# The message stage of a four-layer graph network: high and low halves of the products in the same 96 columns, and Q's rows by a one-hot over 64 rows held twice

## The chip, the cores and the metric

The kernel runs on one core of one Trainium2 chip. The metric is the device time of one execution in microseconds; the kernel before takes 2623.59 us (median of 3 runs, 2621.11 to 2624.36). Times inside an execution come from the hardware profiler. Engines are named as the profile names them: PE (TensorE, its weight loads apart as PEld), DVE (VectorE), ACT (ScalarE), POOL (GpSimd) and SP (SyncE, which here only issues transfers).

## What is computed

The input is a graph of 3125 nodes with 96 features and 100000 edges, sorted by destination, with 4 attributes per edge. Four layers are added to `x` one after the other, each on `relu(layernorm(x))`. The change concerns the third, whose message part is this (cut from the reference):

```python
dst = jnp.minimum((3125 * jax.random.uniform(key3, (100000,)) ** 2.0).astype(jnp.int32), 99999)
_o = jnp.argsort(dst, stable=True)
...
def _mlp(h, W, b, gamma, beta):
    h = jax.nn.relu(h @ W + b)
    mu = jnp.mean(h, axis=0)
    var = jnp.mean(jnp.square(h - mu), axis=0)
    return gamma * (h - mu) * jax.lax.rsqrt(var + EPS) + beta
node_feat = _mlp(x, W_node, b_node, g_node, beta_node)
edge_feat = _mlp(edge_attr, W_edge, b_edge, g_edge, beta_edge)
row, col = (edge_index[0], edge_index[1])
message = jnp.concatenate([x[row], x[col], edge_feat], axis=1)
message = _mlp(message, W_msg, b_msg, g_msg, beta_msg)
agg = jax.ops.segment_sum(message, col, num_segments=node_feat.shape[0])
return agg + node_feat
```

`row` is the source of an edge, `col` its destination. Destinations are denser at low node numbers, and sorted, so that consecutive edges have the same or neighbouring destinations.

## The kernel before

The first layers (edge preparation, ten hops of propagation, softmax aggregation) come ahead of the part that the change touches, and the last layer behind it. One exception: the edge preparation writes tables that the message stage reads later.

**Split numbers.** Products that must be nearly fp32 are made of fp16 numbers: a value is held as a high half and the low remainder. `split` writes both: ACT casts the value to fp16, DVE subtracts the cast from the value (the page's lines L369 and L370).

**Tables.** The message of an edge is relu(P[source] + Q[destination] + edge features x W3), where P and Q are the nodes' products with their parts of the weights. `Pt` and `Qt` hold them in memory, one row of 192 fp16 numbers per node: 96 high and 96 low ones.

**Quads and halves.** The edges are worked in `Q` = 98 quads of `QE` = 1024, each of two halves (`PER` = 2), each half of four chunks (`HC` = 4) of 128 edges. For a quad `load_quad` issues on SP's queue: the 128 rows of `Qt` from the quad's first destination on, into `qg` (the row number comes from the table `rows` in a register); the edge attributes `et`; and `rlb`, every edge's destination relative to the quad's first one, spread over all 128 partitions. `rows_hot` (L741) compares `rlb` with the partition number `part`, which gives the one-hot `ohT` (destination row by edge). `cols_hot` makes the transposed one, `oh`, for the sums.

**Gathers.** `gather_rows(i)` issues on POOL four indirect transfers (L736), each of which brings the `Pt` rows of 128 edges into one of six buffers of a half, `pgs`. A buffer is rewritten when the half six places before has been read by PE.

**One half.** `edge_features` multiplies the attributes on PE into `ef`; ACT's relu gives `eh`, DVE's L757 the rest `el`. `messages(i)` then makes, for each chunk, four matmuls in one PSUM tile `pre` of 192 columns: `eh` times `W3h` (high and low side by side, 192 columns, L766), `el` times the high half (96 columns, L767), `ohT` times `qg` (192, L768), and the identity times the gathered rows (192, L769). The tile holds four chunks at a stride of 256 fp32 columns, which is two PSUM banks, and there are two such tiles. ACT copies the low 96 columns to `mt` (L771), DVE adds the high ones (L772), makes the relu (L774, less the message at the mean, `cb`), and `split` puts both halves in one of four buffers `mms`. Two halves later `summed` multiplies the one-hot `oh` with them on PE (segment sums, L792) and the messages with themselves (their second moments for the normalisation, L794). After a quad's second half its sums go to memory from `sacc` (L797 to L799), and into the next quad's sum (L791).

**Order.** The whole stage is issued in an order written by hand (`manual_schedule`). In turn i: edge features of half i+1, sums of half i-2, messages of half i, `rows_hot` of the next quad in an even turn, `cols_hot` and `load_quad` (two quads ahead) and a piece of the node branch (`node_piece`) in an odd one, then the gathers of half i+5. Each engine runs its instructions in this order.

**Edge preparation.** Destinations relative to the quad's first are computed as `rl` on 98 partitions (a quad each) of 1024 edges; `rlh` is its cast to fp16 (L303), which `rl_d` keeps for `rlb`. `firsti` goes to `row_d`, from which `rows` is loaded. `lo` holds a base row of each group of edges, `rows` in this place the destinations. Sums in the columns of `over` count edges that don't fit the assumed layout; if any is above zero, another, general function does the work (`wide`).

Of the kernel before, what the change touches and what calls it, by code (L numbers as in the profile page):

```python
# [20 lines left out]
P = 128  # L21
N, D, E = 3125, 96, 100000
# [7 lines left out]
HC = 4  # L30
# [8 lines left out]
BN_EPS = 1e-5  # L39
K_HOPS, ALPHA, BETA = 10, 0.1, 0.9  # L40
Q, QE = 98, 1024
ROWS = 4
WIN = 20
PAD = WIN
# [10 lines left out]
def narrow(ctx: ExitStack, tc: tile.TileContext, a: dict, out: bass.AP, flag: bass.AP):  # L55


    nc = tc.nc
    V, S, G, T = nc.vector, nc.scalar, nc.gpsimd, nc.tensor

    const = ctx.enter_context(tc.tile_pool(name="const", bufs=1))
    dram = ctx.enter_context(tc.tile_pool(name="dram", bufs=1, space=DRAM))
# [3 lines left out]
    Qt = dram.tile([NP + P, 2 * D], F16, name="Qt")  # L66
# [2 lines left out]
    rl_d = dram.tile([Q * QE], F16, name="rl_d")  # L69
    srcT_d = dram.tile([P, Q * 8], I32, name="srcT_d")  # L70
    first_d = dram.tile([1, Q], F32, name="first_d")
    row_d = dram.tile([1, Q], I32, name="row_d")
    base_d = dram.tile([Q * ROWS], I32, name="base_d")
    ea_d = dram.tile([18, E], F16, name="ea_d")

# [4 lines left out]
    ident16 = const.tile([P, P], F16, name="ident16")  # L80
# [2 lines left out]
    V.memset(ones, 1.0)  # L83
    lane = const.tile([P, P], F16, name="lane")
    G.iota(lane, pattern=[[1, P]], base=0, channel_multiplier=0, allow_small_or_imprecise_dtypes=True)
    part = const.tile([P, 1], F32, name="part")
    G.iota(part, pattern=[[0, 1]], base=0, channel_multiplier=1, allow_small_or_imprecise_dtypes=True)
    top = const.tile([P, 1], F32, name="top")
    V.memset(top, -float(TOP))
    over = const.tile([P, 80], F32, name="over")  # L90
    V.memset(over, 0.0)
    where = [const]
# [47 lines left out]
    with tc.tile_pool(name="edges", bufs=1) as sp, tc.tile_pool(name="onehot", bufs=3) as hp, tc.tile_pool(name="handed", bufs=2) as hd, \  # L140
# [56 lines left out]
        w = sp.tile([Q, QE], F32, name="w")  # L197
# [102 lines left out]
        turned(rlT, rl)  # L300
        turned(srcT, sb)
        rlh = sp.tile([Q, QE], F16, name="rlh")
        V.tensor_copy(rlh, rl)  # L303
        nc.sync.dma_start(rl_d.rearrange("(q e) -> q e", q=Q), rlh)
        nc.sync.dma_start(rlT_d, rlT.rearrange("p q j -> p (q j)"))
        nc.sync.dma_start(srcT_d, srcT.rearrange("p q j -> p (q j)"))


        firsti = sp.tile([Q, 1], I32, name="firsti")
        V.tensor_copy(firsti, lo[:, 0:1])  # L310
        nc.sync.dma_start(row_d.rearrange("o q -> q o"), firsti)
        nc.sync.dma_start(first_d.rearrange("o q -> q o"), lo[:, 0:1])
        fr = sp.tile([P, Q], F32, name="fr")
        nc.sync.dma_start(fr, first_d.to_broadcast([P, Q]))
# [30 lines left out]
    def over_b(t, nb=NB):  # L345

        return t[:, None, :].to_broadcast([P, nb, D])
# [228 lines left out]
    nc.sync.dma_start(rlT, rlT_d)  # L576
    srow = where[-1].tile([P, Q * 8], I32, name="srow")
    nc.sync.dma_start(srow, srcT_d)
    rows = where[-1].tile([1, Q], I32, name="rows")
    nc.sync.dma_start(rows, row_d)  # L580
    li = where[-1].tile([P, P, 4], F16, name="li2")
    G.iota(li, pattern=[[1, P], [0, 4]], base=0, channel_multiplier=0, allow_small_or_imprecise_dtypes=True)  # L582
# [85 lines left out]
    with tc.tile_pool(name="msg", bufs=1) as lp, tc.tile_pool(name="gath", bufs=6) as gp, \  # L668
# [48 lines left out]
        st = {"acc": None}  # L717

        def load_quad(g):
            r0 = nc.values_load(rows[0:1, g:g + 1], engines=(mybir.EngineType.SP,), min_val=0, max_val=N - 1,  # L720
                                skip_runtime_bounds_check_because="a dst is a node")
            qg = gp.tile([P, 2 * D], F16, name="qg")
            nc.sync.dma_start(qg, Qt[bass.ds(r0, P), :])
            et = wp.tile([18, QE], F16, name="et", bufs=4)
            n = min(QE, E - g * QE)
            if n < QE:
                V.memset(et, 0.0)
            nc.sync.dma_start(et[:, :n], ea_d[:, g * QE:g * QE + n])
            rlb = rlbs[g % len(rlbs)]
            nc.sync.dma_start(rlb, bass.AP(tensor=rl_d.tensor, offset=rl_d.offset + g * QE, ap=[[0, P], [1, QE]]))  # L730
            quad[g] = [r0, qg, et, rlb]
# [6 lines left out]

        def rows_hot(g):
            ohT = wp.tile([P, QE], F16, name="ohT")  # L740
            V.tensor_scalar(ohT, quad[g][3], part, None, ALU.is_equal)  # L741
            quad[g].append(ohT)

        def cols_hot(g):
# [15 lines left out]
        def messages(i):  # L760
            r0, qg, et, rlb, ohT, oh = quad[i // PER]
            eh, el = half_[i]
            ps = p2.tile([P, HC, 256], F32, name="pre")[:, :, :2 * D]
            for c in range(HC):
                cs = slice(c * P, (c + 1) * P)
                T.matmul(ps[:, c, :], eh[:, cs], W3h, start=True, stop=False)  # L766
                T.matmul(ps[:, c, :D], el[:, cs], W3h[:, :D], start=False, stop=False)  # L767
                T.matmul(ps[:, c, :], ohT[:, i % PER * HC * P + c * P:i % PER * HC * P + (c + 1) * P], qg, start=False, stop=False)  # L768
                T.matmul(ps[:, c, :], ident16, pgs[i % len(pgs)][:, c, :], start=False, stop=True)  # L769
            t = wp.tile([P, HC, D], F32, name="mt")  # L770
            S.activation(t, ps[:, :, D:], AF.Copy)  # L771
            V.tensor_add(t, t, ps[:, :, :D])  # L772
            m = wp.tile([P, HC, D], F32, name="m")
            V.scalar_tensor_tensor(m, t, 0.0, over_b(cb, HC), ALU.max, ALU.subtract)  # L774
            for c in range(HC):
                first = E - (i * HC + c) * P
                for p0, pn in ((0, 32), (32, 32), (64, 64)) if first < P else ():
                    assert first <= p0 or first >= p0 + pn
                    if first <= p0:
                        V.memset(m[p0:p0 + pn, c, :], 0.0)  # L780
            mm = mms[i % len(mms)]
            split(mm[:, :, :D], mm[:, :, D + 2:], m)
# [720 lines left out]
```

## Time and profile before

| what | value |
|---|---|
| median of the runs | 2623.59 us |
| the profiled execution | 2623.51 us |
| its span, first to last instruction | 2621.6 us |
| mean granted TensorE clock | 0.813 |
| PE / DVE / ACT / POOL busy, share of the span | 75 / 59 / 37 / 31% |
| message stage, place in the span | about 1256 to 2455 us |
| gathers (L736) | 784, 992 ns each |
| messages' matmuls (L766 to L769) | 4 x 784 |

The page has numbered parts. Its second part cuts the span into 40 slices of 65.5 us; a digit is the busy share of a slice in tenths, and in the clock's row the granted clock in tenths of full speed. Its fifth part lists groups of instructions: line, engine, operation, output and inputs, shapes, count; then busy time and mean duration in ns; then how long the engine had been idle ahead of them and what ended most of that. A timeline gives start, duration, and in brackets the idle time ahead of an instruction with its releaser. Ends of matmuls are modelled, so starts are safer than ends. "issue" is time in which an engine waited for nothing that the profile shows.

### The profile page before, as it was taken

To read this page: it belongs to the slowest core of one execution; us is meant where nothing else is said; L and a number is where in the kernel's file an instruction comes from. 1 tells how busy PE (TensorE), PEld (TensorE's weight loads), DVE (VectorE), ACT (ScalarE), POOL (GpSimd) and SP (SyncE) were. 2 spreads that over 40 slices of the span, in tenths; PEclk is the share of its full clock that TensorE was granted. 3 is DMA by queue.
4 is the path that set the end of the run, shared out by engine and by line. 5 is a ranking of instruction groups with operands and counts; after the bars stand their busy time and mean duration, and the time that the engine had idled before them with its cause. 6 is when DMAs were issued, how large, how long until landed. Compare 5 with 4: busy or idle time off the path is not lost.

```text
span 2621.6 us, 43748 instructions
## 1 busy us (share of the span) xinstructions
PE 1975.0 (75%) x16190; PEld 1516.1 (58%) x16190; DVE 1540.0 (59%) x4164; ACT 959.6 (37%) x2332; POOL 819.6 (31%) x808
## 2 busy tenths in 40 slices
PE   0477777899999999998475566667677767667598
PEld 0222334788888899987354444445455555455488
DVE  2777999875656553877255454445444444445753
ACT  0398855469533311433132222222222222222340
POOL 4000000000000000000666566666666666666000
PEclk9789989999999999999556766765666665676699
DMA  2100000000000000000222222322222223232100
GB/s 66 55 24 1 1 1 1 5 9 10 9 10 10 10 21 2 19 21 18 61 66 67 52 67 65 71 65 70 64 70 66 70 65 70 64 70 66 29 2 21
DMA packets 101315, 100.65 MB, mean 38 GB/s; under 512 B 66285, under 2 KB 73206, under 8 KB 101090
## 3 DMA queue, kind: packets, MB, share of 16 engines
q1 hardware_dynamic: 73754, 54.78, 7.9%
q0 software_dynamic: 25088, 38.59, 7.4%
q10 hardware_dynamic: 2248, 4.40, 0.6%
q8 instruction: 128, 2.10, 0.3%
q14 instruction: 97, 0.79, 0.1%
HBM read 83.46 MB, written 14.21 MB: 37 GB/s over the span
## 4 chain that ended last, share of the span: by engine, by line
PE 44%; DVE 16%; issue 13%; ACT 9%; another core or an unknown queue 1%; DMA 0%; SPq 0%; DVEq 0%; ACTq 0%; POOL 0%; POOLq 0%
PE hop L380 19%; PE segs L792 4%; PE gram L794 3%; PE pre L769 3%; PE pre L768 3%; ACT x L524 3%; DVE u L370 3%; PE pre L766 3%; DVE mt L772 2%; DVE m L774 2%; PE ef L753 2%; ACT mt L771 2%; PE pre L767 1%; PE eps L513 1%; ACT A L437 1%
## 5 line engine op out<-in xcount | busy, mean ns | idle before, releaser
L736 POOL DMA_INDIRECT u<-Pt,srow x784 | 778.0, 992 | 550.8 <-issue 180.2
L380 PE MATMUL hop<-u,A 128*128 128x192 f16 (+1 forms) x6250 | 550.0, 247 | 2.3 <-DVE degs L474 1.4
L380 PEld LDWEIGHTS <-A 128*128 128x128 fp8e4 x6250 | 522.5, 98 | 47.4 <-issue 43.8
L792 PE MATMUL segs<-u,oh 128*128 128x194 f16 x784 | 225.8, 323 | 232.7 <-DVE ohT L741 139.4
L772 DVE TENSOR_TENSOR mt<-mt,pre 128x384 f32<-128x384 f32 x196 | 108.4, 553 | 478.9 <-ACT mt L771 345.6
L771 ACT ACTIVATE mt<-pre 128x384 f32<-128x384 f32 x196 | 96.1, 490 | 605.9 <-PE pre L769 249.6
L768 PE MATMUL pre<-qg,ohT 128*128 128x192 f16 x784 | 256.9, 328 | 25.6 <-issue 25.3
L769 PE MATMUL pre<-u,ident 128*128 128x192 f16 x784 | 258.5, 330 | 22.4 <-issue 21.4
L269 PE MATMUL cps<-hk,hl 128*128 128x500 f16 x784 | 232.7, 418 | 54.1 <-DVE hl L227 35.5
L794 PEld LDWEIGHTS <-u 128*97 128x97 f16 x784 | 137.2, 175 | 235.2 <-issue 231.5
L766 PE MATMUL pre<-W3h,eh 96*128 96x192 f16 x784 | 259.0, 330 | 15.4 <-issue 14.6
L227 DVE TENSOR_TENSOR hk<-ki,keyT 128x4000 f16<-128x4000 f16 x98 | 220.5, 2250 | 45.0 <-PE cps L269 27.5
L794 PE MATMUL gram<-u 128*97 128x194 f16 x784 | 228.2, 325 | 3.7 <-issue 3.5
L767 PE MATMUL pre<-W3h,el 96*128 96x96 f16 x784 | 204.8, 261 | 28.5 <-issue 25.5
L582 POOL IOTA li<- 128x512 f16 x1 | 1.2, 1185 | 680.2 <-ACT exs L500 680.2
L273 ACT ACTIVATE C<-cps 128x500 f32 x269 | 162.8, 605 | 93.2 <-PE cps L272 66.4
L369 ACT ACTIVATE u<-m 128x384 f16<-128x384 f32 x196 | 102.5, 523 | 243.5 <-DVE m L774 204.2
L370 DVE TENSOR_TENSOR u<-m,u 128x384 f16<-128x384 f32 x196 | 109.5, 559 | 115.6 <-issue 86.7
L269 PEld LDWEIGHTS <-hl 128*128 128x128 f16 x784 | 74.0, 119 | 167.6 <-DVE hl L227 76.4
L792 PEld LDWEIGHTS <-oh 128*128 128x128 f16 x784 | 101.5, 129 | 109.4 <-issue 109.4
L514 ACT ACTIVATE eps<-eps 96x512 f32<-96x512 f32 x196 | 106.3, 569 | 154.5 <-PE eps L513 146.0
L515 DVE BATCH_NORM_STATS2 x<-eps 96x6 f32<-96x512 f32 x196 | 134.2, 688 | 30.8 <-ACT eps L514 28.2
(308 smaller groups left out, 3244.3 us busy)
## 6 DMA issues: line engine op xcount, KB each, us to landing
h<-rl_d SPq DMA_DIRECT2D x98, 256.0 KB
u<-Pt,srow POOLq DMA_INDIRECT x784
qg<-Qt SPq DMA_DIRECT2D x98, 48.0 KB
Sd<-sacc SPq DMA_DIRECT2D x98, 48.0 KB
x<-ea_d SPq DMA_DIRECT2D x195, 18.0 KB
et<-ea_d SPq DMA_DIRECT2D x97, 36.0 KB
et<-in_edge_attr_T ACTq DMA_DIRECT2D x4, 390.6 KB
ea_d<-eh SPq DMA_DIRECT2D x8, 195.3 KB
```

Of the source, the lines that this page charges most:

```text
L227: V.tensor_tensor(t, pat[:, None, :, :].to_broadcast([P, s, n, c]), val[:, q, :].rearrange("p (s c) -> p s c", s=s)[:, :, None, :].to_broa ...
L269: T.matmul(ps, hl[:, j // 4, :, j % 4], hk[:, j // 2, :, j % 2], start=j == js[0], stop=n == 0 and j == js[-1])
L273: S.activation(C8[:, :, bass.ds(column_of(g), WIN)], ps, AF.Copy)
L370: V.tensor_sub(lo, t, hi)
L380: T.matmul(ps[:, i, :], table[:, k, c0 + (b0 + i) * P:c0 + (b0 + i + 1) * P], u[:, k, :], start=k == 0, stop=k == NB - 1)
L736: G.indirect_dma_start(out=pgs[i % len(pgs)][:, c, :], out_offset=None, in_=Pt, in_offset=bass.IndirectOffsetOnAxis(ap=srow[:, k:k + 1], a ...
L766: T.matmul(ps[:, c, :], eh[:, cs], W3h, start=True, stop=False)
L767: T.matmul(ps[:, c, :D], el[:, cs], W3h[:, :D], start=False, stop=False)
L768: T.matmul(ps[:, c, :], ohT[:, i % PER * HC * P + c * P:i % PER * HC * P + (c + 1) * P], qg, start=False, stop=False)
L769: T.matmul(ps[:, c, :], ident16, pgs[i % len(pgs)][:, c, :], start=False, stop=True)
L792: T.matmul(seg, oh[:, half, :, c], mm[:, c, :], start=half == 0 and c == 0, stop=last)
L794: T.matmul(gram, mm[:, c, :D + 1], mm[:, c, :], start=i == 0 and c == 0, stop=g == Q - 1 and last)
```

## The change

In `messages` the six products of a chunk, high or low, all go into the same 96 columns: `eh` times the high and the low half of `W3`, `el` times the high half, the one-hot times `qg`, the identity times the high and times the low gathered half. PSUM adds what the copy and the addition added before; `mt` is gone, and `m` reads `pre`, which is one bank for four chunks.

For Q's two halves in one matmul, `qg` holds 64 rows twice: the high halves in partitions 0 to 63, the low ones of the same rows in partitions 64 to 127, and the one-hot has a one in both places (`part_hw` counts 0 to 63 twice). Since 64 rows must do, each half of a quad has its own first row, so `qg` has two blocks, and four transfers of 64 x 96 numbers fill it; two rows per quad are loaded into registers. `rlh` is therefore relative to the half's first row, and an edge that lies 64 or more rows above it is counted in a new column of `over`. The gathers, the sums and the order of issue are as before.

```diff
+HW = 64
...
-    row_d = dram.tile([1, Q], I32, name="row_d")
+    row_d = dram.tile([1, 2 * Q], I32, name="row_d")
...
-    part = const.tile([P, 1], F32, name="part")
-    G.iota(part, pattern=[[0, 1]], base=0, channel_multiplier=1, allow_small_or_imprecise_dtypes=True)
+    part = const.tile([P, 2], F32, name="part")
+    G.iota(part, pattern=[[0, 2]], base=0, channel_multiplier=1, allow_small_or_imprecise_dtypes=True)
+    V.tensor_scalar(part[HW:, 1:2], part[HW:, 1:2], -float(HW), None, ALU.add)
+    part, part_hw = part[:, 0:1], part[:, 1:2]
...
-        V.tensor_copy(rlh, rl)
+        r2 = rlh.rearrange("q (t e) -> q t e", t=2)
+        V.tensor_sub(r2, rows.rearrange("q (a b) e -> q a (b e)", a=2),
+                     lo.rearrange("q (a b) -> q a b", b=2)[:, :, 0:1].to_broadcast([Q, 2, QE // 2]))
+        V.tensor_scalar(bad, rlh, float(HW), None, ALU.is_ge)
+        V.tensor_reduce(over[:Q, 5:6], bad, AX.X, ALU.add)
...
-        firsti = sp.tile([Q, 1], I32, name="firsti")
-        V.tensor_copy(firsti, lo[:, 0:1])
-        nc.sync.dma_start(row_d.rearrange("o q -> q o"), firsti)
+        firsti = sp.tile([Q, 2], I32, name="firsti")
+        V.tensor_copy(firsti, lo.rearrange("q (a b) -> q a b", b=2)[:, :, 0])
+        nc.sync.dma_start(row_d.rearrange("o (q t) -> (o q) t", t=2), firsti)
...
         def load_quad(g):
-            r0 = nc.values_load(rows[0:1, g:g + 1], engines=(mybir.EngineType.SP,), min_val=0, max_val=N - 1,
-                                skip_runtime_bounds_check_because="a dst is a node")
-            qg = gp.tile([P, 2 * D], F16, name="qg")
-            nc.sync.dma_start(qg, Qt[bass.ds(r0, P), :])
+            _, r = nc.values_load_multi_w_load_instructions(
+                rows[0:1, 2 * g:2 * g + 2], engines=(mybir.EngineType.SP,), min_val=0, max_val=N - 1,
+                skip_runtime_bounds_check_because="a dst is a node")
+            r0 = r[0]
+            qg = gp.tile([P, 2, D], F16, name="qg")
+            for t in range(2):
+                for k in range(2):
+                    nc.sync.dma_start(qg[k * HW:(k + 1) * HW, t, :], Qt[bass.ds(r[t], HW), k * D:(k + 1) * D])
...
-            V.tensor_scalar(ohT, quad[g][3], part, None, ALU.is_equal)
+            V.tensor_scalar(ohT, quad[g][3], part_hw, None, ALU.is_equal)
...
-            ps = p2.tile([P, HC, 256], F32, name="pre")[:, :, :2 * D]
+            ps = p2.tile([P, 512], F32, name="pre")[:, :HC * D].rearrange("p (c d) -> p c d", c=HC)
+            pg = pgs[i % len(pgs)]
             for c in range(HC):
                 cs = slice(c * P, (c + 1) * P)
-                T.matmul(ps[:, c, :], eh[:, cs], W3h, start=True, stop=False)
-                T.matmul(ps[:, c, :D], el[:, cs], W3h[:, :D], start=False, stop=False)
-                T.matmul(ps[:, c, :], ohT[:, i % PER * HC * P + c * P:i % PER * HC * P + (c + 1) * P], qg, start=False, stop=False)
-                T.matmul(ps[:, c, :], ident16, pgs[i % len(pgs)][:, c, :], start=False, stop=True)
-            t = wp.tile([P, HC, D], F32, name="mt")
-            S.activation(t, ps[:, :, D:], AF.Copy)
-            V.tensor_add(t, t, ps[:, :, :D])
+                o = ohT[:, i % PER * HC * P + c * P:i % PER * HC * P + (c + 1) * P]
+                for j, (t, w) in enumerate(((eh[:, cs], W3h[:, :D]), (eh[:, cs], W3h[:, D:]), (el[:, cs], W3h[:, :D]),
+                                            (o, qg[:, i % PER, :]), (ident16, pg[:, c, :D]), (ident16, pg[:, c, D:]))):
+                    T.matmul(ps[:, c, :], t, w, start=j == 0, stop=j == 5)
             m = wp.tile([P, HC, D], F32, name="m")
-            V.scalar_tensor_tensor(m, t, 0.0, over_b(cb, HC), ALU.max, ALU.subtract)
+            V.scalar_tensor_tensor(m, ps, 0.0, over_b(cb, HC), ALU.max, ALU.subtract)
```

More of the change, by code (lines that the diff above doesn't have):

```diff
@@ L578, in narrow @@
     nc.sync.dma_start(srow, srcT_d)
-    rows = where[-1].tile([1, Q], I32, name="rows")
+    rows = where[-1].tile([1, 2 * Q], I32, name="rows")
     nc.sync.dma_start(rows, row_d)
```

## The prediction

> **What bounds the kernel now.** I began with the page: the sliced busy rows first, then the groups.
>
> ```profile
> PE   0477777899999999998475566667677767667598
> POOL 4000000000000000000666566666666666666000
> PEclk9789989999999999999556766765666665676699
> ...
> L736 POOL DMA_INDIRECT u<-Pt,srow x784 | 778.0, 992 | 550.8 <-issue 180.2
> L792 PE MATMUL segs<-u,oh 128*128 128x194 f16 x784 | 225.8, 323 | 232.7 <-DVE ohT L741 139.4
> L772 DVE TENSOR_TENSOR mt<-mt,pre 128x384 f32<-128x384 f32 x196 | 108.4, 553 | 478.9 <-ACT mt L771 345.6
> L771 ACT ACTIVATE mt<-pre 128x384 f32<-128x384 f32 x196 | 96.1, 490 | 605.9 <-PE pre L769 249.6
> L768 PE MATMUL pre<-qg,ohT 128*128 128x192 f16 x784 | 256.9, 328 | 25.6 <-issue 25.3
> L767 PE MATMUL pre<-W3h,el 96*128 96x96 f16 x784 | 204.8, 261 | 28.5 <-issue 25.5
> ```
>
> A slice is 65.5 us. POOL works only in slices 20 to 37: this is the message stage (about 1256 to 2455 us of the span), the only place where the change has much to do. Its 1200 us are 98 quads of 1024 edges, two halves of 512 each. No engine is full there, and the granted clock falls to 0.5 to 0.7. Next I asked for the engines' busy times in stretches of the stage, and then for the timelines of one quad, POOL, ACT, PE in turn:
>
> ```profile
> 1850.00:2000.00 150.00, 104.33 (x658) 76.45 (x656) 74.39 (x143) 40.84 (x91) 100.50 (x102) 0.64 0.29 68
> 2000.00:2150.00 150.00, 103.44 (x655) 75.20 (x654) 71.84 (x139) 39.85 (x89) 99.64 (x101) 0.65 0.28 66
> ...
> 2002.55 0.94 POOL L736 DMA_INDIRECT u<-Pt,srow  x1 [1.82 <-PE pre L769]
> ...
> 2011.61 0.95 POOL L736 DMA_INDIRECT u<-Pt,srow  x1 [0.31 <-issue]
> 2014.43 0.94 POOL L736 DMA_INDIRECT u<-Pt,srow  x1 [1.87 <-PE pre L769]
> ...
> 2002.57 0.49 ACT L771 ACTIVATE mt<-pre 128x384 f32<-128x384 f32 x1 [4.76 <-PE pre L769]
> ...
> 2014.44 0.49 ACT L771 ACTIVATE mt<-pre 128x384 f32<-128x384 f32 x1 [4.77 <-PE pre L769]
> ...
> 2009.96 0.37 PE L769 MATMUL pre<-u,ident 128*128 128x192 f16 x1
> ```
>
> (Columns of the stretches: length, then PE, PE load, DVE, ACT, POOL busy, clock, DMA share, GB/s.) Three things are to be seen. First, a quad lasts 2014.43 - 2002.55 = 11.88 us, and POOL fills 10.01 of it with eight gathers (2002.55 to 2012.56, a gather each 1.25 us), then stands for 1.87 us. It stands because the message rows go into six buffers: the next gather may start only when L769 has read the buffer. Second, that L769 had been executed long before: the even half's last one ended at 2010.33 by the trace, and ACT's copy, which waits for nothing else, began at 2014.44, 4.11 us later. Both engines were released in the same moment, 1.9 us after POOL's last gather ended. So completions of PE reach the waiting engines late while gathers are being issued, and in a bunch once POOL stands. Third, the loop behind that moment, from the chain of waits of this window:
>
> ```profile
> 2003.10 0.57 DVE mt L772
> 2003.66 0.02 issue
> 2003.68 0.56 DVE m L774
> 2004.24 0.59 issue
> 2004.83 0.56 DVE u L370
> 2005.39 0.45 DVE ohT L741
> 2005.83 0.80 issue
> 2006.64 0.32 PE segs L792
> ```
>
> From copy to copy the work is: mt copied and added (1.11 us), m, its high and low halves, then the sums of that half on PE (from 2006.64) and the next even half's messages (2007.88 to 2010.33). That is 7.8 us; the rest of the 11.88 is the late signal.
>
> **What the Trainium skill says.** "TensorE: Matmul & The Clock Gate", "Back-to-back issue gap": start to start is the column count over 1.2 GHz while cold and over 2.4 GHz plus about 2.5 ns when warm. The trace agrees for the cold state: 192-column matmuls start 160 ns apart and 96-column ones 80 to 90 ns (2012.82 to 2012.90), the weight load hidden. "VectorE: DVE Perf Modes", "Why PSUM operands drop a tier": with a PSUM operand fp32 runs at the single rate. L774 works on fp32 and three operands already; L772, with one operand in PSUM, takes 553 ns against L774's 560, so I cost m's new source at nothing. "DMA: Bandwidth & Descriptors", "Specifications": below 512 B a transfer is under line rate. The old Q rows (384 B) and the new ones (192 B) are both below; the page counts 66285 of 101315 packets under 512 B already, at a DMA share of 0.28 to 0.29. No section I found bears on signals of PE held up by gathers.
>
> **The change part by part.**
>
> *The copy and the add go.* 196 x 490 = 96.1 us of ACT and 196 x 553 = 108.4 us of DVE. Neither engine is full (40 and 72 of 150 us), so only their place on the chain counts: m starts where the copy started, 1.11 us earlier (2002.57 instead of 2003.68) in each half.
>
> *Fewer columns, more instructions.* A chunk goes from 192+96+192+192 = 672 columns in four matmuls to 6 x 96 = 576 in six. At the cold spacing a half's messages take 24 x 0.08 = 1.92 us instead of 4 x 0.56 = 2.24: 0.32 us less, if an instruction costs only its columns. PE gets 16 pairs of load and matmul more per quad (1568 of each in all). An unknown is what a pair costs where completions are held up; below, rival S.
>
> *One PSUM bank for a half instead of two, still two buffers.* They come free after m rather than after the add, which is the same moment or 0.5 us earlier. Nothing.
>
> *Signals.* In the compiled program PE's messages carry fewer completions: most of the plain ones sat on ohT and ident matmuls of the 192-column form and fall away (per quad about 21 before, 11 after; POOL still needs one per gather). If each costs a turn at a narrow place, this helps; waits on PE rise by two per quad. Below nothing, up to rival G.
>
> *Q rows.* Per quad four loads of 64 x 192 B instead of one of 128 x 384 B, and six more SP instructions. SP issues at 2006.61, 2008.35 and 2009.07 in this quad and rests otherwise: a qg issue has a median of 26 ns, a register move 29 ns, so 6 x 0.03 = 0.2 us on an idle queue, with load_quad two quads ahead. The row loads of rlb stand behind them by that 0.1 to 0.2 us; rows_hot needs them more than 10 us later. Cost nothing; if the cover were gone, 0.2 us per quad, 20 us. DMA bytes are the same; 128 more small packets beside some 1024 of gathers per quad.
>
> *One-hot and edges phase.* L741 is the same instruction with another scalar. In the edges phase the cast of 0.69 us (L303) becomes a subtraction (nearest row 1.22 us, L296), and a compare (0.69, L288) and a reduce (1.22, L287) are new: +2.4 us on DVE, which is near full there, so I count all of it, plus 0.1 us for the small part column. The flag that it fills rises only if a half spans 64 rows or more: destinations are 3125 u² with u uniform and sorted, so the widest half is the last, 3125 x (1 - (1 - 0.00512)²) = 32 rows. So it isn't raised.
>
> *The sum.* The chain of a quad is shorter by 1.11 + 0.32 = 1.43 us: the even half's first gather buffer is read at about F + 4.9 instead of F + 6.1 (2008.65 against the release at 2002.55), and all four by F + 6.3 instead of 7.8. POOL runs out at F + 10.0 as before. Whether the completion comes before that decides. Half of the stop is what I take as likeliest: a signal that is ready earlier and has fewer beside it gets through in some quads before POOL stands and in others not. The stop is 1.87 - 0.30 = 1.57 us beyond the ordinary pause between gathers; with it gone a quad would be 10.31 us. Half is 0.8 us in 83 regular quads: -66 us. In the ten or so quads with a node piece (1410 to 1530; POOL busy 69 of 120 us against 100 of 150) PE waits for DVE and ACT and the late signal is not the limit, so the chain counts in full: 10 x 1.43 = -14; the first quads, where the first 28 gathers are issued without a reader, and the last two: -4. Edges +2.5. Sum -82 us against the profiled execution's 2623.51 us (span 2621.6), which is 0.1 us from the median of 2623.59: 2542 us.
>
> **The rivals.**
>
> *G, POOL becomes the only bound.* The stop goes in all regular quads: 83 x 1.57 = -130, with the other terms -146: 2478 us. For it: the completions halve and come 1.4 us earlier. Against: held-up completions have been seen to pass only when POOL stands, and if it no longer stands they may pile up. Chance 0.24.
>
> *P, the stop stays.* The quad is eight gathers and the time to drain, whatever the chain does; only node pieces, first and last quads gain: -16 us, 2607 us. For it: release comes at a fixed 1.9 us after the last gather (2000.73 to 2002.55, 2012.56 to 2014.43), though L769 had ended 4 us earlier. Then a shorter chain is worth nothing. If the edges phase or Q loads take a little more, it ends within 5 us of before (a third of this case). Chance 0.21.
>
> *S, slower: PE is paid by the instruction.* Where completions are held up, PE's matmuls stall as well (L766 at 2013.40 was followed by L767 at 2014.10: 0.70 us for an 80 to 160 ns step). Mean durations show how little the columns count: 261 ns for 96 (L767), 328 for 192 (L768). If a half's messages are worth 24 x 0.261 = 6.3 us instead of 12 x 0.329 + 4 x 0.261 = 5.0, PE loses 1.3 us per half against the 1.1 us won by the copy and the add; both halves lie in PE's order one behind the other, 2.6 lost against 2.2 won, and PE's 8.2 us busy per quad become 10.8, more than the 10.3 of POOL. One 0.7-us stall more per quad beside that, for the two added waits, makes about +0.9 to +1.1 us per quad: 2623.5 + 95 = 2720 us. It decides from about 0.23 us per added pair. Without that stall it would be +0.4 us per quad, 2662 us. Chance 0.22.
>
> **How the numbers follow.** Half of the stop gone 0.33, G 0.24, P 0.21, S 0.22. The time is that of the likeliest, 2542 us; its own range is 2500 to 2585 (a quarter to nearly all of the stop gone, the unknown costs within). For eight in ten the range goes from 2460 (G with a little more in the node pieces) to 2655 (S where PE keeps most of its cover). A change within 0.2% (5 us) is about what a measurement of this kernel can't tell from none. Faster: 0.33 + 0.24 + two thirds of P = 0.71; same 0.07; slower 0.22.
>
> **What would show it.** In the changed kernel's POOL timeline the idle time before every eighth gather: 1.8 us again means P, 0.3 means G, a mixture or an intermediate value my forecast. m's start against the last ident matmul of its half gives the late signal (4.1 us now). PE's busy time per 150 us above 125 and 96-column matmuls starting more than 0.2 us apart would be S. If the time changes outside 1256 to 2455 us by more than 5 us, my reading of the edges phase was wrong.

## The result and the profile after

The changed kernel is slower: 2651.11 us (median of 4 runs, 2647.15 to 2655.02) against 2622.35 us for the kernel before, a ratio of 1.011 with a 95% interval of 1.0092 to 1.0128. The forecast was 2542 us, faster.

From the page of the changed kernel, the sliced rows and the groups of the message stage (a group's last two numbers are the idle time ahead of it and what ended most of it):

```profile
PE   0477777899999999997475666767776776667699
POOL 4100000000000000000666566666666666666000
PEclk9889999999999999998566675556555556555599
...
L747 POOL DMA_INDIRECT u<-Pt,srow x784 | 766.9, 978 | 590.3 <-issue 186.4
L783 DVE SCALAR_TENSOR_TENSOR m<-pre,cb 128x384 f32<-128x384 f32 x196 | 109.1, 557 | 577.6 <-PE pre L781 287.1
L781 PE MATMUL pre<-u,ident 128*128 128x96 f16 x1568 | 275.8, 267 | 68.9 <-issue 68.0
L781 PE MATMUL pre<-W3h,eh 96*128 96x96 f16 x1568 | 279.8, 269 | 58.4 <-issue 56.9
```

The change did what its text says: copy and addition are gone, and m takes 557 ns from PSUM (560 ns before). The stage is still 784 gathers in 18 slices, and POOL's idle time ahead of them rose from 550.8 to 590.3 us. Now the busy times by stretch (columns as in the prediction), then POOL's timeline:

```profile
1850.00:2000.00 150.00, 108.06 (x864) 81.29 (x862) 55.26 (x109) 26.60 (x60) 96.76 (x100) 0.55 0.27 66
2000.00:2150.00 150.00, 105.96 (x834) 77.36 (x834) 57.61 (x112) 27.98 (x62) 95.85 (x99) 0.56 0.27 68
```

```profile
2004.65 0.94 POOL L747 DMA_INDIRECT u<-Pt,srow  x1 [1.86 <-PE ef L764]
...
2013.63 0.94 POOL L747 DMA_INDIRECT u<-Pt,srow  x1 [1.47 <-remote]
...
2022.75 0.95 POOL L747 DMA_INDIRECT u<-Pt,srow  x1 [1.75 <-remote]
```

DVE and ACT work less (57 and 28 us of 150, before 72 and 40), and nobody gains: 99 to 100 gathers pass per 150 us instead of 101 to 102. POOL stands after six gathers here. Over the steady stretch from 1540 to 2300 us I counted its pauses above 0.6 us: 59 before, of 1.84 us each, mostly eight gathers apart; 93 in the changed kernel, of 1.54 us, mostly five to seven apart; 108 against 144 us in all. In this stretch 514 gathers began before and 502 in the changed kernel, so a gather with its share of the pauses took 1.479 and 1.514 us. Over 784 gathers the difference makes 27 us (an estimate from these two figures), about the 29 us that the change cost. PE's timeline ahead of the second pause shown above is this:

```profile
2009.37 0.21 PE L781 MATMUL pre<-qg,ohT 128*128 128x96 f16 x1
2009.42 0.20 PE L781 MATMUL pre<-u,ident 128*128 128x96 f16 x1
2010.49 0.20 PE L781 MATMUL pre<-u,ident 128*128 128x96 f16 x1 [0.86 <-issue]
2010.53 0.21 PE L781 MATMUL pre<-W3h,eh 96*128 96x96 f16 x1
2011.94 0.20 PE L781 MATMUL pre<-W3h,eh 96*128 96x96 f16 x1 [1.21 <-issue]
2011.99 0.20 PE L781 MATMUL pre<-W3h,el 96*128 96x96 f16 x1
2012.69 0.20 PE L781 MATMUL pre<-qg,ohT 128*128 128x96 f16 x1 [0.50 <-issue]
2013.41 0.24 PE L781 MATMUL pre<-u,ident 128*128 128x96 f16 x2 [0.52 <-issue]
```

PE starts matmuls 40 ns apart, and then in the middle of a half it stops, with nothing that the profile shows to wait for: the starts are 1.07, 1.41, 0.70 and 0.72 us apart, until POOL stands (its last gather ended at 2012.15). The waits of PE sum this up. Lines of before first (engine, line, released by: us in total, times, longest), then the line of the changed kernel:

```profile
PE pre L767 <- issue: 25.5, 44, 2.6
PE pre L768 <- issue: 25.3, 49, 1.1
PE pre L769 <- issue: 21.4, 40, 1.6
PE pre L766 <- issue: 14.6, 26, 1.8
```

```profile
PE pre L781 <- issue: 185.1, 255, 1.9
```

86.8 us of unexplained PE idle time inside the messages became 185.1.

### The profile page after: what moved, and what is told of

Same layout as the page of the kernel before. It is cut to its first block, busy times and chain, and to the rows that moved or that the text cites. A ratio compares the mean times of both kernels' runs of the same rounds, so it can differ in the third digit from the quotient of the medians.

```text
span 2645.2 us, 47376 instructions
## 1 busy us (share of the span) xinstructions
PE 2003.1 (76%) x17758; PEld 1553.0 (59%) x17758; DVE 1433.2 (54%) x3971; ACT 870.8 (33%) x2136; POOL 808.4 (31%) x808
## 4 chain that ended last, share of the span: by engine, by line
PE 39%; issue 18%; DVE 14%; ACT 8%; another core or an unknown queue 5%; SPq 0%; DMA 0%; ACTq 0%; DVEq 0%
PE hop L387 19%; PE pre L781 7%; PE segs L801 3%; DVE u L377 3%; ACT x L531 3%; ACT u L376 2%; PE gram L803 2%; DVE el L768 2%; PE ef L764 2%; DVE m L783 1%; PE eps L520 1%; ACT A L444 1%; PE hop L623 1%; DVE oh L757 1%
## 5 line engine op out<-in xcount | busy, mean ns | idle before, releaser
L747 POOL DMA_INDIRECT u<-Pt,srow x784 | 766.9, 978 | 590.3 <-issue 186.4
L783 DVE SCALAR_TENSOR_TENSOR m<-pre,cb 128x384 f32<-128x384 f32 x196 | 109.1, 557 | 577.6 <-PE pre L781 287.1
L801 PE MATMUL segs<-u,oh 128*128 128x194 f16 x784 | 239.6, 337 | 126.3 <-issue 76.1
L781 PE MATMUL pre<-u,ident 128*128 128x96 f16 x1568 | 275.8, 267 | 68.9 <-issue 68.0
L781 PE MATMUL pre<-W3h,eh 96*128 96x96 f16 x1568 | 279.8, 269 | 58.4 <-issue 56.9
L803 PE MATMUL gram<-u 128*97 128x194 f16 x784 | 245.4, 344 | 5.4 <-issue 5.4
L230 DVE TENSOR_TENSOR hk<-ki,keyT 128x4000 f16<-128x4000 f16 x98 | 220.3, 2248 | 43.7 <-PE cps L272 27.2
L781 PE MATMUL pre<-qg,ohT 128*128 128x96 f16 x784 | 210.2, 268 | 33.0 <-issue 32.9
L781 PE MATMUL pre<-W3h,el 96*128 96x96 f16 x784 | 210.1, 268 | 30.4 <-issue 27.2
L781 PEld LDWEIGHTS <-eh 96*128 96x128 f16 x1568 | 178.4, 136 | 77.1 <-issue 74.5
L803 PEld LDWEIGHTS <-u 128*97 128x97 f16 x784 | 143.2, 183 | 123.2 <-issue 118.9
L781 PEld LDWEIGHTS <-ident 128*128 128x128 f16 x1568 | 164.9, 135 | 74.0 <-issue 73.9
```

The costliest lines, as they stand in the source:

```text
L230: V.tensor_tensor(t, pat[:, None, :, :].to_broadcast([P, s, n, c]), val[:, q, :].rearrange("p (s c) -> p s c", s=s)[:, :, None, :].to_broa ...
L747: G.indirect_dma_start(out=pgs[i % len(pgs)][:, c, :], out_offset=None, in_=Pt, in_offset=bass.IndirectOffsetOnAxis(ap=srow[:, k:k + 1], a ...
L781: T.matmul(ps[:, c, :], t, w, start=j == 0, stop=j == 5)
L783: V.scalar_tensor_tensor(m, ps, 0.0, over_b(cb, HC), ALU.max, ALU.subtract)
L801: T.matmul(seg, oh[:, half, :, c], mm[:, c, :], start=half == 0 and c == 0, stop=last)
L803: T.matmul(gram, mm[:, c, :D + 1], mm[:, c, :], start=i == 0 and c == 0, stop=g == Q - 1 and last)
```

## The experiments

**The loss depends on where one measures.** The kernel before itself came out in two ways. Kernels measured together shared one chip and the runs of before; five such sessions followed.

| session | before, us | kernels: ratio to before, 95% interval |
|---|---|---|
| 1 | 2437.1 | split_only 1.0005 (0.9995 to 1.0015), newq_only 0.995 (0.9933 to 0.9966), qg_two 0.9968 (0.9958 to 0.9979), four_products 0.9943 (0.9926 to 0.9959) |
| 2 | 2438.1 | after_again 0.9951 (0.9932 to 0.997); one execution each: no_gather_after 2029.46 us, no_gather_before 2165.45 us, before_again 2441.13 us |
| 3 | 2614.3 | after_third 1.0085 (1.0069 to 1.0102), split_only_b 1.0043 (1.0027 to 1.0059), newq_only_b 1.0019 (1.0004 to 1.0035), qg_two_b 1.0073 (1.0048 to 1.0098) |
| 4 | 2625.35 | p_on_dve 1.0182 (1.0151 to 1.0213), p_on_dve3 1.0303 (1.0273 to 1.0333), four_products_b 0.9988 (0.9975 to 1.0); one execution: no_gather_after_b 2046.1 us |
| 5 | 2630.54 | six_copy 1.0148 (1.0121 to 1.0174), after_fourth 1.0077 (1.005 to 1.0104) |

Sessions 3 to 5 are like the measurement; I call them held-up, and 1 and 2 free. The listed number of the chip was the same in sessions 1 and 3, so I don't call this a property of a chip. Ratios of different sessions are less comparable than their intervals say: the same changed kernel had 1.011 in the measurement, 1.0085 in session 3 and 1.0077 in session 5.

**Session 1: parts.** I had two theories of the PE stalls. A: PE's instructions bring them on, since there are 24 pairs of load and matmul per half instead of 16. B: SP's transfers do. The edit of split_only cuts two products of before in two:

```diff
-                T.matmul(ps[:, c, :], ohT[:, i % PER * HC * P + c * P:i % PER * HC * P + (c + 1) * P], qg, start=False, stop=False)
-                T.matmul(ps[:, c, :], ident16, pgs[i % len(pgs)][:, c, :], start=False, stop=True)
+                o = ohT[:, i % PER * HC * P + c * P:i % PER * HC * P + (c + 1) * P]
+                T.matmul(ps[:, c, :D], o, qg[:, :D], start=False, stop=False)
+                T.matmul(ps[:, c, D:], o, qg[:, D:], start=False, stop=False)
+                T.matmul(ps[:, c, :D], ident16, pgs[i % len(pgs)][:, c, :D], start=False, stop=False)
+                T.matmul(ps[:, c, D:], ident16, pgs[i % len(pgs)][:, c, D:], start=False, stop=True)
```

> The kernel before, with its one-hot and its gathered products (192 columns) each cut into two of 96: 24 pairs of load and matmul per half as in the changed kernel, but 672 columns per chunk, the copy, the addition and the single Q load kept. Theory A (a PE instruction is what fills something while gathers run, so that PE stalls earlier in a run of gathers): about 2690 us or more, PE stalls from the fourth or fifth gather of a run on. Theory B (SP's transfers do it: four Q loads of 0.75 us each instead of one): 2620 to 2635 us, stalls from the eighth gather on as before.

newq_only is the changed kernel with before's products put back, and only the new Q rows kept (the added lines):

```diff
...
+                T.matmul(ps[:, c, :], eh[:, cs], W3h, start=True, stop=False)
+                T.matmul(ps[:, c, :D], el[:, cs], W3h[:, :D], start=False, stop=False)
+                T.matmul(ps[:, c, :D], ohT[:, i % PER * HC * P + c * P:i % PER * HC * P + (c + 1) * P], qg[:, i % PER, :], start=False, stop=False)
+                T.matmul(ps[:, c, :], ident16, pgs[i % len(pgs)][:, c, :], start=False, stop=True)
...
+            S.activation(t, ps[:, :, D:], AF.Copy)
+            V.tensor_add(t, t, ps[:, :, :D])
```

> The changed kernel with before's four matmuls per chunk for all but Q (eh and identity products 192 wide, copy and addition kept); Q by the doubled one-hot of 64 rows and four loads per quad: 16 pairs per half, 576 columns. Theory A (PE instructions): 2590 to 2620 us, PE stalls from the eighth gather of a run on, POOL standing once in eight gathers. Theory B (SP's transfers): 2680 us or more, stalls from the fourth to sixth gather on.

qg_two is the changed kernel, but loads both copies of a half's rows in one transfer:

```diff
-                for k in range(2):
-                    nc.sync.dma_start(qg[k * HW:(k + 1) * HW, t, :], Qt[bass.ds(r[t], HW), k * D:(k + 1) * D])
+                nc.sync.dma_start(qg[:, t, :], Qt[bass.ds(r[t], HW), :].rearrange("r (k d) -> k r d", k=2))
```

> The changed kernel with one Q load per half (both copies of the rows in one transfer) instead of two: two per quad, same bytes and packets. Theory A: as the changed kernel, 2640 to 2655 us. Theory B: half of the loss of the Q loads comes back, 2580 us or less, and SP's row of Q loads takes 1.5 us per quad instead of 3.2.

four_products is the changed kernel without two products of a chunk, so its sums lack these parts:

```diff
-                for j, (t, w) in enumerate(((eh[:, cs], W3h[:, :D]), (eh[:, cs], W3h[:, D:]), (el[:, cs], W3h[:, :D]),
-                                            (o, qg[:, i % PER, :]), (ident16, pg[:, c, :D]), (ident16, pg[:, c, D:]))):
-                    T.matmul(ps[:, c, :], t, w, start=j == 0, stop=j == 5)
+                for j, (t, w) in enumerate(((eh[:, cs], W3h[:, :D]), (el[:, cs], W3h[:, :D]),
+                                            (o, qg[:, i % PER, :]), (ident16, pg[:, c, :D]))):
+                    T.matmul(ps[:, c, :], t, w, start=j == 0, stop=j == 3)
```

> The changed kernel without two of its six products per chunk (edge features by the low half of W3, identity by the low gathered half are left out): 16 pairs per half, 384 columns, no copy, no addition, four Q loads. Theory A: about 2480 us, POOL nearly never stands. Theory B: no more than 30 us below the changed kernel, 2620 us, since the transfers stay.

None of these numbers was met; all four lie within 15 us of a kernel before that is itself 185 us quicker than in the measurement. POOL never stands in the steady stretch of any of them. So they say nothing on A and B, but show another bound.

**Session 2: the changed kernel where nothing is held up, and without gathers.**

> The changed kernel itself, beside the kernel before, on the chip of these runs. In the first runs of this study the kernel before took 2437 us on a chip where POOL never stood, against 2622 us in the measurement of the change. Theory C (two conditions of the chip: where completions and transfers are held up while gathers run, the change costs 1%; where they aren't, POOL's gathers are the bound and the change is worth little either way): if before is near 2437 us, the changed kernel is within 15 us of it, below rather than above, and POOL stands nowhere in the steady part; if before is near 2622 us, the changed kernel is near 2650 us with POOL standing every 5 to 7 gathers. Rival (the change costs PE time of its own): 20 us or more above before in both.

> The kernel before, for its trace on the chip of these runs. Near 2437 us: POOL's gathers follow one another every 1.25 to 1.28 us without standing, and the copy L771 begins within 0.3 us of the end of the last identity matmul of its half. Near 2622 us: POOL stands 1.8 us after eight gathers, the copy begins 3 to 4 us late.

Both came out as theory C had it. The POOL timeline of before in session 2, and after it the two kernels' gather groups (before, then changed):

```profile
2000.68 0.94 POOL L736 DMA_INDIRECT u<-Pt,srow  x1 [0.30 <-PE pre L769]
2001.92 0.95 POOL L736 DMA_INDIRECT u<-Pt,srow  x1 [0.30 <-PE pre L768]
```

```profile
L736 POOL DMA_INDIRECT u<-Pt,srow x784 | 769.2, 981 | 391.7 <-DMA Qt<-hv 153.0
```

```profile
L747 POOL DMA_INDIRECT u<-Pt,srow x784 | 759.1, 968 | 391.9 <-DMA Qt<-hv 153.3
```

POOL goes from gather to gather with 0.30 us between. The copy (or m) begins 0.04 us after the end of the last identity matmul of its half in the median, where it was 3.9 us in the measurement, in both kernels. The chain has slack. The change is worth 12 us here (2425.89 against 2438.12); the two traced executions differ by 15.0 us, 10.1 of which are gathers that take 968 instead of 981 ns. This gain doesn't come from the copy and the addition: newq_only, which keeps both, had the same ratio in session 1 (0.995 against 0.9951), with gathers of 965 ns. What shortens a gather I didn't test. In the changed kernel each of the 55 gathers above 1.0 us between 1540 and 2200 us overlaps DVE's `oh` or `ohT`, but in the kernel before only 37 of 65 do, and in both most of the gathers that overlap them stay below 1.0 us.

Then the gathers were left out after the first six halves, with one edit in either kernel, so that the rows of `Pt` are stale:

```diff
-            for c in range(HC):
+            for c in range(HC) if i < len(pgs) else ():
                 k = i * HC + c
```

> The changed kernel with the gathers of the first six halves alone; the later ones are left out, so that POOL issues nothing in the steady part and the six buffers are read again and again. Theory C and theory A or B: PE's completions arrive at once, no PE stalls of 0.7 us, a quad takes what the chain and PE need, 7 to 8 us: stage 700 to 800 us, 2150 to 2250 us in all, on whatever chip. Rival (the held-up completions come from the matmuls themselves): quads of 10 us and more, stalls as with gathers.

> The kernel before with the gathers of the first six halves alone. With the gathers gone the chain is all that is left, and here the copy and the addition are on it: 0.5 to 1.5 us per quad more than in the changed kernel without gathers, so 50 to 150 us more in all. If it is the same or less, the copy and the addition were never worth anything, in no condition of the chip.

2029.46 against 2165.45 us: the change is worth 136.0 us, 1.39 us per quad on average, once POOL is out of the way, as expected of the kernel before. A quad takes 5.58 us in the median, 6.76 before. The changed kernel itself is quicker than I expected (2150 to 2250 us, 7 to 8 us per quad). In its stretches without gathers PE is the busiest engine, 128 of 150 us, at full clock:

```profile
1500.00:1650.00 150.00, 128.12 (x1832) 104.56 (x1831) 118.25 (x242) 57.94 (x135) 0.00 (x0) 1.00 0.30 73
```

**Session 3: the parts again, held up.**

> The changed kernel again, since two chips so far (before at 2437 and 2438 us) differ from the one of the measurement (2622 us). Theory C: it goes with the kernel before of the same chip: near 2425 us where before is near 2438, near 2650 where before is near 2622. Rival (the difference between 1.011 and 0.995 is chance from run to run): any pairing of these.

> Only of use if before is near 2622 us here. Theory A (PE's instructions bring on the held-up state): 2680 us or more, PE stalls from the fourth or fifth gather of a run on. Theory B (SP's Q loads do): 2610 to 2635 us, stalls from the eighth gather on. Where before is near 2437 us: within 10 us of it, as before.

> Only of use if before is near 2622 us here. Theory A: 2590 to 2620 us, POOL standing once in eight gathers or more. Theory B: 2660 us or more, POOL standing every 5 to 7 gathers. Where before is near 2437 us: about 2425 us, as before.

> Only of use if before is near 2622 us here. Theory A: 2640 to 2660 us, as the changed kernel. Theory B: 20 to 60 us below the changed kernel. Where before is near 2437 us: about 2430 us, as before.

The ratio above 1 of the change is no chance. B fell, though split_only_b lies in its range: the new Q rows with their four loads cost 0.19%, and half of the changed kernel's loads gave nothing that the intervals separate (1.0073 against 1.0085), though SP needs 3.0 to 3.2 us for four. A had the direction and not the size: splitting costs 0.43%, 11 us, where 65 or more were expected. PE's unexplained waits in split_only_b, six groups now, and in newq_only_b:

```profile
PE pre L772 <- issue: 28.2, 31, 3.3
PE pre L770 <- issue: 23.7, 37, 1.9
PE pre L769 <- issue: 20.9, 34, 2.6
PE pre L771 <- issue: 20.4, 28, 3.3
PE pre L767 <- issue: 18.7, 25, 2.5
PE pre L766 <- issue: 16.8, 19, 1.9
```

```profile
PE pre L779 <- issue: 24.8, 31, 2.6
PE pre L780 <- issue: 23.0, 35, 2.6
PE pre L778 <- issue: 19.4, 27, 2.5
PE pre L777 <- issue: 16.5, 23, 2.5
```

128.7 us with 24 pairs, 83.7 with 16, near before's 86.8. In proportion to the pairs 86.8 would become 130. The onset follows the pairs too. Counted from the moment when POOL starts again, the first stall above 0.45 us among the message products, where one comes before POOL stands, comes in the median after 10.8 us and 49 of PE's matmuls in the kernel before, 10.1 us and 48 in newq_only_b, 7.2 us and 59 in split_only_b, 5.3 us and 44 in the changed kernel (5.8 us and 52 in after_third). The times differ by a factor of two, the numbers of matmuls much less.

**Session 4: fewer pairs.** If pairs are what counts, taking the gathered rows off PE should help. p_on_dve is the changed kernel with this edit (m then reads `t`):

```diff
-                                            (o, qg[:, i % PER, :]), (ident16, pg[:, c, :D]), (ident16, pg[:, c, D:]))):
-                    T.matmul(ps[:, c, :], t, w, start=j == 0, stop=j == 5)
+                                            (o, qg[:, i % PER, :]))):
+                    T.matmul(ps[:, c, :], t, w, start=j == 0, stop=j == 3)
+            t = wp.tile([P, HC, D], F32, name="mt")
+            V.tensor_add(t, ps, pg[:, :, :D])
+            V.tensor_add(t, t, pg[:, :, D:])
```

> The changed kernel with the gathered rows added by DVE (two additions of 128 x 384 per half) instead of two identity products per chunk: 16 pairs per half, 384 columns. Theory A (PE's instruction supply): on a chip where before is near 2615 us about 2540 to 2590 us, stalls from the seventh gather on or never. Rival (the state is set by the gathers' time alone, pairs don't matter): 2630 us or more, for DVE's additions are 1.1 us more on the chain. Where before is near 2438 us: 2425 to 2435 us, POOL's bound.

In p_on_dve3 the edge features are again one product of 192 columns, and DVE adds three times (some of the added lines):

```diff
...
+                T.matmul(ps[:, c, :], eh[:, cs], W3h, start=True, stop=False)
...
+            S.activation(t, ps[:, :, D:], AF.Copy)
+            V.tensor_add(t, t, pg[:, :, D:])
+            V.tensor_add(t, t, pg[:, :, :D])
+            V.tensor_add(t, t, ps[:, :, :D])
```

> As p_on_dve, but the edge features times both halves of W3 in one matmul of 192 columns, with the copy of the low ones and one more addition on DVE: 12 pairs per half. Theory A: the least held-up of all, 20 to 50 us below p_on_dve on a chip where before is near 2615 us. Rival (the chain of DVE's additions decides): above p_on_dve by 50 us or more, since 0.5 us of copy and 0.55 us of addition are added per half. Where before is near 2438 us: 2425 to 2440 us.

> Leaves out the products with the low half of W3 and the low gathered half; 16 pairs, 384 columns, no copy or addition. Theory A, where before is near 2615 us: 2520 to 2580 us, for the copy's 1.1 us per half are won without more PE instructions. Rival (removing the copy and the addition is worth nothing in that state): 2605 us or more. Where before is near 2438 us: 2423 us as before.

> The changed kernel with the gathers of the first six halves alone, on another chip. Theory A says that it is the gathers that starve PE: also where before is near 2615 us no stalls and no late completions, 2025 to 2040 us as on the first kind of chip. Rival (PE on that chip is slow by itself): 2080 us or more.

All three fell on A's wrong side: p_on_dve by 82 us, four_products_b by 42, and p_on_dve3 is 34 us above p_on_dve where 20 to 50 less were expected. The stalls did what A said: PE waits 73.4 us in p_on_dve's messages for "issue", 95 times, and POOL runs twelve gathers before it stands. But it then stands 2.75 us, a gather costs 1.56 us with its share of the pauses (1.48 before), and the time goes up. With the same pairs and columns, four_products_b has no additions and is 50 us below p_on_dve, so work between the end of the products and m does count in this state.

Yet four_products_b itself has as many pairs as the kernel before, 288 fewer columns per chunk, no copy and no addition, and is only 3 us faster (0.9988). The gap from the end of a half's last message matmul to m is 5.7 us in the median, where it was 3.9 in the measurement: what PE finishes earlier waits longer.

Without gathers the same changed kernel takes 2046.1 us in session 4, 16.6 us more than in session 2 and 6 more than I had expected at most. From its trace, PE, then POOL's last gather, then DVE's first m, and last PE's waits of the whole execution:

```profile
1264.27 0.25 PE L781 MATMUL pre<-W3h,eh 96*128 96x96 f16 x1 [0.52 <-issue]
1265.72 0.24 PE L781 MATMUL pre<-W3h,el 96*128 96x96 f16 x1 [1.20 <-issue]
1267.86 0.24 PE L781 MATMUL pre<-qg,ohT 128*128 128x96 f16 x1 [1.90 <-issue]
...
1280.07 0.95 POOL L747 DMA_INDIRECT u<-Pt,srow  x1 [0.30 <-issue]
...
1285.64 0.56 DVE L783 SCALAR_TENSOR_TENSOR m<-pre,cb 128x384 f32<-128x384 f32 x1 [25.51 <-remote]
...
PE pre L781 <- issue: 9.4, 7, 1.9
```

While the 24 gathers that are left run, from 1251.1 to 1281.0 us, PE stalls and completions are late: the first half's last matmul ended at 1261.53, and its m began 24.1 us later, 4.6 us after POOL's last gather. In session 2 it began 0.04 us after the matmul. All of the 9.4 us lie before 1285 us (the changed kernel with gathers has 175 to 203 in its held-up executions), and a quad then takes 5.58 us in the median as in session 2. By the sixth half the kernel is 15.1 us behind the one of session 2, which is most of the 16.6. So in this one held-up execution PE is held up while gathers run, and not otherwise.

**Session 5: the sign of the copy at 24 pairs.** six_copy is newq_only with the gathered product cut in three (`pg` is the half's buffer):

```diff
-                T.matmul(ps[:, c, :], ident16, pgs[i % len(pgs)][:, c, :], start=False, stop=True)
+                T.matmul(ps[:, c, :D], ident16, pg[:, c, :D], start=False, stop=False)
+                T.matmul(ps[:, c, D:D + D // 2], ident16, pg[:, c, D:D + D // 2], start=False, stop=False)
+                T.matmul(ps[:, c, D + D // 2:], ident16, pg[:, c, D + D // 2:], start=False, stop=True)
```

> The changed kernel's Q rows, 24 pairs and 576 columns per chunk as there (192, 96, 96, 96, 48, 48), but low and high columns apart, with the copy and the addition. If the parts add up (13 and 4 us), 15 to 20 us above before where before is near 2615 to 2625 us, and the changed kernel is above it: then taking the copy away doesn't help and may cost. If the copy and addition are worth something in that state, it is 10 us or more above the changed kernel. Where before is near 2438 us: within 10 us of 2430, POOL's bound.

> The changed kernel beside six_copy on the same chip. Where before is near 2615 to 2625 us: 1.008 to 1.011 of before. Where before is near 2438 us: 0.995.

The changed kernel is 17.9 us below six_copy (2667.87 against 2650.0): even held up, the copy and the addition are a gain when they go. The two also differ in the widths of the pieces and in the space that they take in PSUM, which I didn't take apart. With 16 pairs the same step, and 192 fewer columns, gave 0.3 percentage points (newq_only_b 1.0019, four_products_b 0.9988, of different sessions) where it gave 0.7 here, so what the copy and the addition are worth depends on the rest. The first expectation failed: six_copy is 37 us above before and not 15 to 20. And eight pairs more per half cost more here than in split_only_b: from newq_only_b to six_copy the ratio rises by 1.3 percentage points, about 34 us, with the columns the same. These two are of different sessions, each against its own before. PE's stalls don't tell the two apart: six_copy's messages have 131.1 us of unexplained waits, split_only_b's 128.7. So the sum of the stalls isn't the price: 42 us more than before in one, 47 more than newq_only_b in the other, and the time rose by 11 and by about 34 us.

The balance of the change, held up, is then: Q's rows +0.2% (newq_only_b), pairs +1.3% (six_copy over newq_only_b), copy and addition -0.7% (after_fourth under six_copy). The sum is the +0.8% of after_fourth by construction; the measurement had +1.1%. In session 3 the two parts measured beside after_third, +0.2% and split_only_b's +0.4%, leave +0.2% of its +0.85% for the copy and the addition, and not -0.7%. So the sizes of the parts are not settled.

## Why the prediction was wrong

- **The step that failed** is "Half of the stop is what I take as likeliest", -66 us. The stop did not shrink. In the steady stretch POOL stood 93 times instead of 59, for 144 us instead of 108. An earlier completion is not an earlier signal: m began 3.9 us after its half's last matmul in the median, as the copy had before, and in four_products_b, without the added pairs, 5.7 us. Nor do held-up completions pass only when POOL stands, as the prediction took it: in the steady stretch of before 57 of 129 copies begin in a pause of POOL, and the other 72 while gathers run, 3.1 us late in the median. In the changed kernel 81 of 126 begin in a pause.
- **The second one** is "0.32 us less, if an instruction costs only its columns". I saw the 0.7-us stalls and put them into rival S, but the forecast itself priced 16 more pairs per quad at nothing. They cost 0.43% (split_only_b) to 1.3% (six_copy over newq_only_b). S had the mechanism, PE stalls, and a price too high: 95 us against 11 to 34. It also named two added waits as a cause, which no run tests; the stalls fall on all kinds of products (the page's groups have 68.0 us ended by "issue" on the gathered rows, 56.9 on `eh`, 32.9 on `qg`, 27.2 on `el`).
- **Signals.** That fewer completions would pass more easily did not show: the changed kernel has the same median of 3.9 us.
- **P**, the stop stays, was nearest on why nothing is won. Its fixed release did not hold (POOL stood 1.54 us on average instead of 1.84, and more often), and it missed that the pairs would be a loss.
- **The chain.** My 1.43 us per quad are near the 1.39 without gathers, but this is luck in part. The sum was made for one half of a quad at the low clock of the held-up loop; without gathers the clock is full, the loop is another, and the medians of a quad differ by 1.18 us. In the free sessions the gain was hidden by POOL's gathers, and in the held-up ones by the stop and the pairs.
- **The spacing** that the prediction takes from the Trainium skill ("TensorE: Matmul & The Clock Gate", "Back-to-back issue gap") is stated there for an isolated matmul, not for a stream of weight loads and matmuls. The traces bear it out for the stream: 80 to 90 ns for 96 columns at the low clock, and 43 ns on average in the changed kernel without gathers, at full clock.
- **m's new source** cost nothing, as said. **Q rows**: I took 26 ns for the issue of a load from before; the four took 3.0 to 3.2 us per quad on SP. That stayed nearly hidden: with all four, newq_only_b is 0.19% above before.
- **Edges phase.** +2.5 us is too little to be seen against the spread of the stage's start (first gather at 1252.4 us before, 1248.8 in the changed kernel).

What stays open: what the held-up condition is, why its step is 0.7 us, why the changed kernel stalls more (175 to 203 us) than split_only_b and six_copy with as many pairs, and whether POOL's issuing or the gathers' transfers cause it. That PE's supply of instructions runs dry would fit an onset after 40 to 60 matmuls, but p_on_dve, with 76 matmuls to its first stall, doesn't fit a fixed supply. The trace also records loads of 16 KB of instructions, on the queue that has 13 more of them in the changed kernel: one each 22.4 us in the steady stretch, taking 1.06 us in the median, and 1.10 us in the free session. Of the 176 stalls above 0.45 us between message products there, 11 overlap such a load, about what chance would give, and 2 end within 0.2 us of its end. So these loads don't explain the stalls; the rest is argued and not shown.

## What to carry to other kernels

Before work is taken off a chain, look at what ends the wait behind it. Here m waited for a signal that came late, and not when the matmul ended, so an earlier matmul won nothing. Where an engine already stalls for no visible reason, price added instructions by these stalls and not by the columns alone: eight pairs more per half added 42 to 47 us of stalls here, and 11 to 34 us of time. And ask for the trace of the kernel before a second time on another day: a bound that is only there in some sessions changes the sign of an edit.

## What the runs showed of the hardware

The kernel before took 2437 to 2438 us in two sessions and 2614 to 2631 us in three and in the measurement; by the traces the stage with gathers takes the whole difference (1197.6 against 1013.9 us from its first to its last message work on PE). In the slower condition the copy on ACT, or m on DVE, began 3.9 us in the median after the matmul that it waited for (0.04 us in the free one), and PE stopped between matmuls for about 0.7 us or longer. Both were seen only while gathers ran: with 24 gathers left, the changed kernel's first m was 24.1 us late, and once they had ended a quad took 5.58 us in both conditions.
